# A relational graph network on one core: tail groups of 4 and 7 tiles, shared gather buffers, and accumulators that begin with the bias

## The chip, the cores and the metric

The kernel runs on one core of a Trainium2 chip. A core has five engines with their own instruction queues: TensorE (PE, matrix multiplications, with the loading of its stationary operand shown as PEld), VectorE (DVE), ScalarE (ACT), GpSimd (POOL) and SyncE (SP, which only issues transfers here). They work on SBUF, an on-chip memory of 128 partitions, and on PSUM, where TensorE writes its results, and wait for each other by semaphores. The metric is the time of one execution in microseconds. The kernel before takes 4633.61 us, the median of 10 runs (4629.92 to 4639.09).

## The reference

Two layers of a relational graph convolution over 12,500 nodes of 128 features and 200,000 edges of 10 relations, then a residual and a layer normalisation. The edges are sorted by destination. An edge's relation is the greatest of 10 of its 42 attributes.

```python
def _rgcn_layer(x, src, dst, edge_type, w_rel, root, bias):
    N = x.shape[0]
    seg = dst * NUM_REL + edge_type
    xs = x[src]
    sums = jax.ops.segment_sum(xs, seg, num_segments=N * NUM_REL)
    cnt = jax.ops.segment_sum(jnp.ones(seg.shape, x.dtype), seg, num_segments=N * NUM_REL)
    mean = (sums / jnp.maximum(cnt, 1.0)[:, None]).reshape(N, NUM_REL, -1)
    return jnp.einsum('nrd,rdo->no', mean, w_rel) + x @ root + bias

h = jax.nn.relu(_rgcn_layer(x, src, dst, edge_type, w_rel1, root1, b1))
x = _layernorm(x + _rgcn_layer(h, src, dst, edge_type, w_rel2, root2, b2))
```

So a layer gathers 200,000 rows of 512 bytes, averages them per node and relation, multiplies each average by its relation's 128x128 matrix, and adds the node's own row times `root` and a bias.

## The kernel before

**Tiles and groups.** A tile is 128 edges in order of destination; there are 1,563 tiles. Groups of 16 tiles (`G`) are the unit of work: 95 of them (`NS`), indices 0 to 94, and then a tail of 43 tiles in smaller groups. `groups` (L68 to L72) cuts it into 8, 8, 8, 8, 4, 4 and 3 tiles, indices 95 to 101.

**What a group does**, for each layer:
- `gather` (L464): one indirect transfer per tile, issued by POOL (L466), fetches the 128 source rows into a buffer `g` of 16 tiles. `gpool` has three such buffers, handed out in turn to the groups; a group of 8, 4 or 3 tiles takes a whole one too. The first gather of a group waits until PE is done with the group that had the buffer before, three groups back.
- `ones` (L475): per tile DVE builds a matrix `oh` (L481), with a column for each pair of relation and destination in the tile's window of 12 nodes, holding the edge's weight, and for the group `at` (L485), which places windows among 160 nodes. `dpool` has two buffers for `oh`.
- `sums` (L488): PE multiplies the gathered rows by `oh`, two instructions per tile (L495), into `zp`; ACT copies `zp` to `zs` (L509), one copy per four tiles. There is one `zp`.
- `project` (L514): for each half group of up to 8 tiles 10 relations are summed in `pp` (L521), two instructions each: 40 instructions for a group of 16, 20 for a smaller one. ACT copies the result to `ms` (L527, or L525 when the group is not a whole number of halves).
- `add` (L532): PE places the result among 160 nodes (L537) and DVE adds it to `acc` (L543), the accumulator of all nodes, at an offset read from memory. `pp` is also the name of that PSUM tile, and it has one buffer.

**Blocks of nodes.** When enough groups have been added that a block of nodes is complete (`done_after`, L79), it is finished: 23 blocks of 512 nodes, five of 128 and one of 84. `block_in` (L394) loads the block's rows and transposes them on PE (L407) and copies them on ACT (L409). `block_rows` (L412) adds the bias to the block's part of `acc` on DVE, giving `a` (L416), zeroes that part of `acc` in layer 0 (L418) so that layer 1 can use it, and lets PE add the rows times `root` (L421) and `a`, transposed by the identity (L422). In layer 0 (`hidden`) ACT applies the relu (L435) and SP stores the block to DRAM as `hD`; layer 1 gathers from there. In layer 1 (`final`) DVE and ACT do the residual and the layer normalisation (L447 to L457) and SP stores the output.

**The order** is that of the program as `layer` (L545) writes it out. In the groups of 16 the stages of several groups overlap: a group's gathers run while its predecessors are multiplied and projected. In the tail (`end`) each group is multiplied, projected and added before the next is begun, except that the one-hots of the next group come ahead. The large blocks end with the first groups of the tail; the six small ones are finished after indices 93, 94, 95, 97, 99 and the last. The last block's inputs are loaded early (`ready`). Layer 1's first gather needs the whole of `hD`.

**The beginning.** The edges' data are brought to one column per tile (`sources`, `places`, `types`, `count`), in chunks of 128 tiles, the first ahead of the loop and the others between groups. Ahead of the loop the accumulator is zeroed by 25 copies on ACT (L615), and `weights_in` loads the matrices and biases.

A second, general way through the problem follows behind a flag (from L647), for edges that don't fit the windows. It isn't taken with these inputs.

Of the kernel before, what the change touches and what calls it, by code (L numbers as in the profile page):

```python
# [9 lines left out]
F32 = mybir.dt.float32  # L10
BF16 = mybir.dt.bfloat16
I32 = mybir.dt.int32
AF = mybir.ActivationFunctionType
ALU = mybir.AluOpType
# [6 lines left out]
P = 128  # L21
# [5 lines left out]
G = 16  # L27
QB = 4
HT = 8
# [5 lines left out]
CT = 128  # L35
YB = 512
W = 128
GT = 125
# [5 lines left out]
def rgcn_resnorm_kernel(ctx: ExitStack, tc: tile.TileContext, x, src, dst, attr, w_rel1, root1, b1,  # L44
# [14 lines left out]
    nc = tc.nc  # L59
    N, C = x.shape  # L60
    E = src.shape[0]
    D = attr.shape[1]
    CE = CT * P
    NT = -(-E // P)
# [3 lines left out]
    groups = [(t, G) for t in range(0, NS * G, G)]  # L68
    t = NS * G
    while t < NT:  # L70
        groups.append((t, min(HT if NT - t > 3 * QB else QB, NT - t)))
        t += groups[-1][1]  # L72
    NG = len(groups)
    NPAD = N + SW
# [12 lines left out]
        return min(a + n for a, n in groups if a + n >= t)  # L87

    HALF = NT * P - E
    assert C == P and E % GT == 0 and 0 < HALF < P and NT % CT and 1 < groups[-1][1] < groups[-2][1]  # L90

    const = ctx.enter_context(tc.tile_pool(name="const", bufs=1))
    dram = ctx.enter_context(tc.tile_pool(name="dram", bufs=1, space=DRAM))
    fin = ctx.enter_context(tc.tile_pool(name="fin", bufs=1))
# [12 lines left out]
    gpool = fast.enter_context(tc.tile_pool(name="gpool", bufs=RING))  # L107
# [6 lines left out]
    ident = const.tile([P, P], F32, name="ident")  # L114
# [29 lines left out]
    def later(ins):  # L144

        for f in ahead:
            tc.add_manual_dep(ins.ins, f.ins.name, behind, reason="the first counts wait for it")
# [3 lines left out]
    def then(engine, ins):  # L151

        if engine in loaded:
            loaded.remove(engine)
            tc.keep_in_program_order(ins)
        return ins
# [10 lines left out]
    def sources(c):  # L167
        p = chunk_rows(c)
        s_i = prep.tile([P, P], I32, name="s_i")
        rows_from(s_i, src, c, 0, P)  # L170
        s_f = prep.tile([P, P], F32, name="s_f")
        early(c, nc.vector.tensor_copy(s_f[:p], s_i[:p]))
        return to_edges(idxE, s_f, c)
# [54 lines left out]
    acc = const.tile([P, NPAD], F32, name="acc")  # L228
# [10 lines left out]
    while k < NG:  # L239
        t, n = groups[k]  # L240
# [4 lines left out]
        m = n if q < NG else n - 1  # L245
# [8 lines left out]
    def places():  # L254
        early(0, nc.vector.tensor_scalar(bt, bt, 0, N - 1, op0=ALU.max, op1=ALU.min))
        early(0, nc.vector.tensor_copy(b8, b8_i))
        pw = ps_f.tile([P, YB], F32, name="pf")
        for h in range(2):
            nc.tensor.matmul(pw[:HR, h * NG:(h + 1) * NG], rank[:, h * HR:(h + 1) * HR], b8, start=True, stop=True)
        nc.vector.tensor_scalar(place, pw[:HR, :2 * NG].rearrange("p (h g) -> p h g", h=2), within, None, op0=ALU.add)  # L260
        nc.vector.tensor_reduce(wide[:HR], place, axis=AX.XY, op=ALU.max)

    wsb, rsb, bsb = [], [], []

    def weights_in():
        for l, (wr, ro, bi) in enumerate(((w_rel1, root1, b1), (w_rel2, root2, b2))):
            t = const.tile([P, NREL, C], F32, name=f"w{l}")
            later(nc.sync.dma_start(t, wr.rearrange("r d o -> d r o")))
            wsb.append(t)
            t = const.tile([P, C], F32, name=f"root{l}")  # L270
            later(nc.sync.dma_start(t, ro))
            rsb.append(t)
            t = const.tile([P, 1], F32, name=f"b{l}")
            later(nc.sync.dma_start(t, bi.rearrange("(c o) -> c o", o=1)))
            bsb.append(t)
# [102 lines left out]
    def block(k):  # L378
        n0 = starts[k]
        n = (starts + [N])[k + 1] - n0  # L380
        return n0, n, [(t, min(P, n - t * P)) for t in range(-(-n // P))]
# [12 lines left out]
    def block_in(k, l):  # L394
# [14 lines left out]
        nc.scalar.activation(fT[:, :n], pt[:, :n], AF.Copy)  # L409
        return xb, fT  # L410

    def block_rows(fT, k, l):  # L412

        n0, n, subs = block(k)
        a = fin.tile([P, YB], F32, name="a")
        nc.vector.tensor_scalar(a[:, :n], acc[:, n0:n0 + n], bsb[l], None, op0=ALU.add)  # L416
        if l == 0:
            nc.vector.memset(acc[:, n0:n0 + n], 0.0)  # L418
        pr = ps_f.tile([P, 4, C], F32, name="pf")
        for t, h in subs:  # L420
            nc.tensor.matmul(pr[:h, t, :], fT[:, t * P:t * P + h], rsb[l], start=True, stop=False)  # L421
            nc.tensor.matmul(pr[:h, t, :], a[:, t * P:t * P + h], ident, start=False, stop=True)  # L422
        return pr

    def spans(k):
# [3 lines left out]
    def hidden(k, ready):  # L429

        xb, fT = ready
        pr = block_rows(fT, k, 0)
        hb = fin.tile([P, 4, C], F32, name="hb")
        for p, s in spans(k):
            nc.scalar.activation(hb[:p, s], pr[:p, s], AF.Relu)  # L435
        rows_dma(hb, hD, k, True)
# [24 lines left out]

    HELD = "clamped to a node on the chip"

    def gather(table, t0, n):  # L464
        g = gpool.tile([P, G, C], F32, name="g")
        return g, [then("POOL", nc.gpsimd.indirect_dma_start(  # L466
            out=g[:, j, :], out_offset=None, in_=table, in_offset=bass.IndirectOffsetOnAxis(
                ap=idxE[:, t0 + j:t0 + j + 1], axis=0))) for j in range(n)]
# [139 lines left out]
        yield  # L608

    sources(1)  # L610
    zero = fin.tile([P, YB], F32, name="a")
    nc.vector.memset(zero, 0.0)
    for a in range(0, NPAD, YB):
        m = min(NPAD - a, YB)
        nc.scalar.activation(acc[:, a:a + m], zero[:, :m], AF.Copy)  # L615
    places()
    for _ in chain(types(0), count(0)):
        pass
    weights_in()
    todo = []  # L620
    for c in range(1, NCH):
        s = [as_steps(sources, c + 1)] if c + 1 < NCH else []
# [31 lines left out]
    def relations(ty, dt):  # L654
        o = gp.tile([P, RS], dt, name="rel" + ("b" if dt == BF16 else "f"))
        nc.vector.tensor_scalar(o, iota[:, :RS], ty, None, op0=ALU.is_equal)
        return o
# [53 lines left out]
    def g_before(table):  # L711
        def before(e, ty):
            rel = relations(ty, F32)
            pt = gps.tile([P, P], F32, name="gpt")
            nc.tensor.transpose(pt[:RS], rel, ident)
            relT = gp.tile([RS, P], F32, name="grelT")
            nc.scalar.activation(relT, pt[:RS], AF.Copy)
            v = gp.tile([P, 1], F32, name="gv")
            nc.vector.memset(v, 0.0)
            s_i = gp.tile([P, 1], I32, name="gs_i")  # L720
            nc.sync.dma_start(s_i[:GT], src[ds(e, GT)].rearrange("(e o) -> e o", o=1))
            g = gp.tile([P, C], F32, name="gg")
            nc.vector.memset(g, 0.0)
            nc.gpsimd.indirect_dma_start(out=g[:GT], out_offset=None, in_=table,
                                         in_offset=bass.IndirectOffsetOnAxis(ap=s_i[:GT], axis=0))
            return relT, v, g, ty
        return before
# [12 lines left out]
    def g_messages(l):  # L740
        def messages(st):
            _, v, g, ty = st
            nc.vector.tensor_scalar(v, v, 1.0, None, op0=ALU.max)
            nc.vector.reciprocal(v, v)
            pm = gps.tile([P, C], F32, name="gpm")
            for r in range(NREL):
                vr = gp.tile([P, 1], F32, name="gvr")
                nc.vector.tensor_scalar(vr, ty, float(r), v, op0=ALU.is_equal, op1=ALU.mult)
                gr = gp.tile([P, C], F32, name="ggr")
                nc.vector.tensor_scalar(gr, g, vr, None, op0=ALU.mult)  # L750
                pt = gps.tile([P, P], F32, name="gpt")
                nc.tensor.transpose(pt, gr, ident)
                gT = gp.tile([P, P], F32, name="ggT")
                nc.scalar.activation(gT, pt, AF.Copy)
                nc.tensor.matmul(pm, gT, wsb[l][:, r, :], start=(r == 0), stop=(r == NREL - 1))
            ms = gp.tile([P, C], F32, name="gms")
            nc.scalar.activation(ms, pm, AF.Copy)
            return ms
        return messages
# [8 lines left out]
    with tc.If(flag > 0):  # L768
        nc.vector.memset(acc, 0.0)
        each_tile(lambda e, ty: relations(ty, BF16), [(g_count, None)])  # L770
        nc.sync.dma_start(counts, acc[:RS])
        for l, (table, finish) in enumerate(((x, hidden), (hD, final))):
            nc.vector.memset(acc, 0.0)
            each_tile(g_before(table), [(g_look, g_messages(l)), (g_add, None)])
            for k in range(NBLK):
                finish(k, block_in(k, l))
# [26 lines left out]
```

## Time and profile before

| What | Value |
|---|---|
| median of 10 runs | 4633.61 us (4629.92 to 4639.09) |
| profiled execution | 4627.56 us, of which 4625.8 us span |
| mean granted TensorE clock | 0.753 |
| layer 0's tail, from the first gather of index 95 to the first gather of layer 1 | 2229.01 to 2323.13, 94.1 us |
| layer 1's tail, from the first gather of index 95 to the end | 4519.94 to 4625.8, 105.9 us |
| gathers per layer | 1563, one per 1.25 us within a burst |

Times in the profile are microseconds from the span's start. A burst is a run of gathers on POOL with no wait in it. In the page, an engine's line gives busy time, share of the span and instructions, and the chain of work that ended last is given as shares by engine and by line. An answer by windows has one line per stretch of time: its ends, its length, the busy time of the engine with the number of instructions begun in it, the clock that was granted to TensorE as a share of the full one, the mean busy share of the core's transfer engines, and GB/s. A line of the waits has the engine and line that waited, what it waited for, the time in all, how many times, and the longest.

### The profile page before, as it was taken

How to read it: one execution, taken by the hardware profiler on the slowest of the kernel's cores; microseconds unless marked ns; L12 is line 12 of the kernel's file. 1: busy time of each engine (PE TensorE's matmuls, PEld its weight loads, DVE VectorE, ACT ScalarE, POOL GpSimd, SP SyncE). 2: the span in 40 equal slices, each digit the busy share in tenths (PEclk: the TensorE clock that was granted, in tenths of full speed). 3: DMA queues.
4: the chain of work that ended last, by engine and by line, in shares of the span. 5: the costliest groups of instructions: out<-in, count | busy, mean ns of one | idle time of the engine just before them, and what ended most of it. 6: DMA issues, size and time to landing. Idle time of an engine off the chain costs nothing.

```text
span 4625.8 us, 43799 instructions
## 1 busy us (share of the span) xinstructions
PE 2748.8 (59%) x16206; PEld 2451.9 (53%) x16206; DVE 1513.8 (33%) x4660; ACT 530.0 (11%) x1142; POOL 2965.7 (64%) x3142
## 2 busy tenths in 40 slices
PE   3655655655656566566736556666565565656666
PEld 2445555555555555555625555555555555555556
DVE  4243333333333333333322222222222223222233
ACT  1111111111111111111101111111111111111111
POOL 6666666666666666666566666666666666666663
PEclk7677777777777777777867777777777777777778
DMA  4122222222122121111111111211121112111111
GB/s 138 52 71 78 63 66 80 63 64 76 55 78 75 52 80 51 57 50 52 48 51 51 53 53 52 60 53 53 53 60 53 53 53 60 53 49 53 57 54 40
DMA packets 180538, 278.99 MB, mean 60 GB/s; under 512 B 55608, under 2 KB 127175, under 8 KB 177191
## 3 DMA queue, kind: packets, MB, share of 16 engines
q0 software_dynamic: 100032, 205.07, 15.4%
q1 hardware_dynamic: 78577, 71.03, 4.8%
q8 instruction: 132, 2.16, 0.2%
q14 instruction: 89, 0.73, 0.0%
q10 hardware_dynamic: 1708, 0.01, 0.0%
HBM read 262.28 MB, written 13.60 MB: 60 GB/s over the span
## 4 chain that ended last, share of the span: by engine, by line
issue 26%; PE 26%; POOL 25%; another core or an unknown queue 18%; DVE 5%; ACT 1%; DMA 0%; DVEq 0%; ACTq 0%; POOLq 0%
POOL g L466 25%; PE pp L521 14%; PE zp L495 8%; DVE oh L481 3%; PE pp L537 2%; PE pf L422 1%; PE pf L421 1%; ACT zs L509 1%; PE pf L366 0%; PE pf L364 0%; DVE acc L543 0%; DVE at L485 0%; DVE eqb L362 0%; PE pf L407 0%
## 5 line engine op out<-in xcount | busy, mean ns | idle before, releaser
L521 PE MATMUL pp<-w,zs 128*96 128x128 f32 x7880 | 1507.7, 349 | 1068.3 <-issue 970.7
L466 POOL DMA_INDIRECT g<-in_x_dram,idxE x1563 | 1479.9, 947 | 821.2 <-issue 428.0
L466 POOL DMA_INDIRECT g<-hD,idxE x1563 | 1482.9, 949 | 814.5 <-issue 455.9
L521 PEld LDWEIGHTS pp<-w,zs 128*96 128x96 f32 x7880 | 1324.3, 221 | 1262.1 <-issue 1155.4
L481 DVE TENSOR_SCALAR oh<-bank,keyE,wE 128x120 f32<-128x120 f32 x3126 | 1003.1, 391 | 1104.1 <-remote 966.4
L495 PE MATMUL zp<-oh,g 128*128 128x120 f32 x6252 | 924.4, 299 | 311.9 <-issue 288.7
L495 PEld LDWEIGHTS zp<-oh,g 128*128 128x128 f32 x6252 | 866.1, 215 | 326.7 <-issue 317.7
L509 ACT ACTIVATE zs<-zp 128x480 f32<-128x480 f32 (+1 forms) x782 | 385.5, 574 | 2525.8 <-remote 2356.2
L543 DVE TENSOR_TENSOR acc<-acc,pp 128x160 f32 x204 | 65.6, 322 | 1231.4 <-remote 743.7
L537 PE MATMUL pp<-at,ms 96*128 96x160 f32 (+1 forms) x788 | 172.0, 343 | 276.5 <-issue 232.6
L537 PEld LDWEIGHTS pp<-at,ms 96*128 96x128 f32 (+1 forms) x788 | 122.9, 202 | 316.2 <-issue 261.9
L527 ACT ACTIVATE ms<-pp 96x256 f32<-96x256 f32 (+1 forms) x198 | 74.5, 376 | 921.5 <-remote 544.0
L422 PE MATMUL pf<-ident,a 128*128 128x128 f32 x392 | 95.3, 323 | 97.8 <-issue 64.8
L362 DVE TENSOR_TENSOR eqb<-pf,kh 128x1344 bf16<-128x1344 f32 (+2 forms) x65 | 100.3, 1550 | 114.0 <-PE pf L366 65.9
L485 DVE TENSOR_SCALAR at<-bank,place 96x160 f32<-96x160 f32 x394 | 133.0, 371 | 0.0
L422 PEld LDWEIGHTS pf<-ident,a 128*128 128x128 f32 x392 | 70.7, 222 | 105.0 <-issue 66.0
L421 PE MATMUL pf<-root,fT 128*128 128x128 f32 x388 | 90.5, 315 | 36.3 <-issue 29.1
L447 DVE TENSOR_TENSOR v<-pf,xb 128x512 f32<-128x512 f32 (+1 forms) x28 | 17.4, 620 | 252.0 <-remote 246.1
L421 PEld LDWEIGHTS pf<-root,fT 128*128 128x128 f32 x388 | 70.7, 224 | 42.3 <-issue 33.5
L364 PE MATMUL pf<-eqb,identb 128*128 128x512 bf16 (+2 forms) x130 | 53.2, 409 | 15.8 <-DVE eqb L362 10.0
L435 ACT ACTIVATE hb<-pf 128x512 f32<-128x512 f32 (+2 forms) x29 | 15.4, 532 | 371.3 <-remote 266.1
L366 PE MATMUL pf<-eqb,identb 128*128 128x512 bf16 (+2 forms) x130 | 53.2, 409 | 3.6 <-issue 3.3
(107 smaller groups left out, 454.9 us busy)
## 6 DMA issues: line engine op xcount, KB each, us to landing
m<-in_edge_attr_dram SPq DMA_DIRECT2D x24, 1344.0 KB
g<-in_x_dram,idxE POOLq DMA_INDIRECT x1563
g<-hD,idxE POOLq DMA_INDIRECT x1563
xb<-in_x_dram SPq DMA_DIRECT2D x46, 256.0 KB
hD<-hb SPq DMA_DIRECT2D x23, 256.0 KB
hb<-hD SPq DMA_DIRECT2D x23, 256.0 KB
out_dram<-o SPq DMA_DIRECT2D x23, 256.0 KB
w<-in_L_gnn_w_rel_dram SPq DMA_DIRECT2D x2, 640.0 KB
```

Of the source, the lines that this page charges most:

```text
L362: nc.vector.tensor_tensor(eq[:p], kp[:p, None, :R].to_broadcast([p, DB, R]), fore, op=ALU.is_equal)
L421: nc.tensor.matmul(pr[:h, t, :], fT[:, t * P:t * P + h], rsb[l], start=True, stop=False)
L422: nc.tensor.matmul(pr[:h, t, :], a[:, t * P:t * P + h], ident, start=False, stop=True)
L466: return g, [then("POOL", nc.gpsimd.indirect_dma_start(out=g[:, j, :], out_offset=None, in_=table, in_offset=bass.IndirectOffsetOnAxis(ap= ...
L481: then("DVE", nc.vector.tensor_scalar(oh[:, j, :], iotaP[:, :KW], keyE[:, t:t + 1], wE[:, t:t + 1], op0=ALU.is_equal, op1=ALU.mult))
L485: nc.vector.tensor_scalar(at[:, h, :], iotaP[:HR], place[:, h, k:k + 1], None, op0=ALU.is_equal)
L495: m = nc.tensor.matmul(zp[:, j // QB, j % QB * KW:(j % QB + 1) * KW], g[:, j, :], oh[:, j, :], start=True, stop=True)
L509: then("ACT", nc.scalar.activation(zs[:, :, b * QB:b * QB + m, :], zp[:, b, :m * KW].rearrange("c (j r n) -> c r j n", r=NREL, n=WN), AF.C ...
L521: nc.tensor.matmul(po[:m * WN, h], zs[:, r, h * HT:h * HT + m].rearrange("c j n -> c (j n)"), wsb[l][:, r, :], start=(r == 0), stop=(r == ...
L527: nc.scalar.activation(ms[:, :n // HT], po[:HR, :n // HT], AF.Copy)
L537: nc.tensor.matmul(pa, ms[:m * WN, h], at[:m * WN, h], start=(h == 0), stop=(h == len(parts) - 1))
L543: nc.vector.tensor_tensor(acc[:, s], acc[:, s], pa, op=ALU.add)
```

## The change

Three things are changed.

- The tail's groups: a group of 8 while more than 12 tiles are left, one of 4 while more than 8 are left, then the rest. That makes 8, 8, 8, 8, 4, 7 (indices 95 to 100), 101 groups in place of 102.
- `gather`: a buffer `g` of 16 tiles is taken only when the group begins at a multiple of 16 tiles; other groups write to the rest of the last one. So indices 95 and 96, 97 and 98, and 99 and 100 share a buffer, and only the first of each pair waits for a buffer, that of group 92, 93 and 94.
- The bias: the accumulator is filled with the first layer's bias (25 activations on ACT with the bias as operand, behind `weights_in` now), `block_rows` gives the accumulator itself to PE, and in layer 0 ACT refills the block's part with the second layer's bias behind PE's reading it, ahead of the relu. The addition L416 and the memset L418 go. `zero` becomes a constant tile. The general way's memset becomes a copy of the bias.

```diff
     while t < NT:
-        groups.append((t, min(HT if NT - t > 3 * QB else QB, NT - t)))
+        n = NT - t
+        groups.append((t, HT if n > HT + QB else QB if n > HT else n))
         t += groups[-1][1]
...
+    zero = const.tile([P, YB], F32, name="zero")
+
     def block_rows(fT, k, l):
 
         n0, n, subs = block(k)
-        a = fin.tile([P, YB], F32, name="a")
-        nc.vector.tensor_scalar(a[:, :n], acc[:, n0:n0 + n], bsb[l], None, op0=ALU.add)
-        if l == 0:
-            nc.vector.memset(acc[:, n0:n0 + n], 0.0)
         pr = ps_f.tile([P, 4, C], F32, name="pf")
         for t, h in subs:
             nc.tensor.matmul(pr[:h, t, :], fT[:, t * P:t * P + h], rsb[l], start=True, stop=False)
-            nc.tensor.matmul(pr[:h, t, :], a[:, t * P:t * P + h], ident, start=False, stop=True)
+            nc.tensor.matmul(pr[:h, t, :], acc[:, n0 + t * P:n0 + t * P + h], ident, start=False, stop=True)
+        if l == 0:
+            nc.scalar.activation(acc[:, n0:n0 + n], zero[:, :n], AF.Identity, bias=bsb[1])
         return pr
...
+    shared = {}
+
     def gather(table, t0, n):
-        g = gpool.tile([P, G, C], F32, name="g")
+
+        o = t0 % G
+        if not o:
+            shared["g"] = gpool.tile([P, G, C], F32, name="g")
+        g = shared["g"][:, o:o + n]
         return g, [then("POOL", nc.gpsimd.indirect_dma_start(
             out=g[:, j, :], out_offset=None, in_=table, in_offset=bass.IndirectOffsetOnAxis(
                 ap=idxE[:, t0 + j:t0 + j + 1], axis=0))) for j in range(n)]
...
     sources(1)
-    zero = fin.tile([P, YB], F32, name="a")
     nc.vector.memset(zero, 0.0)
-    for a in range(0, NPAD, YB):
-        m = min(NPAD - a, YB)
-        nc.scalar.activation(acc[:, a:a + m], zero[:, :m], AF.Copy)
     places()
     for _ in chain(types(0), count(0)):
         pass
     weights_in()
+    for a in range(0, NPAD, YB):
+        m = min(NPAD - a, YB)
+        nc.scalar.activation(acc[:, a:a + m], zero[:, :m], AF.Identity, bias=bsb[0])
```

## The prediction

> **What bounds the kernel now.** I read the page's busy times and its chain first, then TensorE's (PE's) instruction counts window by window, then the waits and the chain at the ends of the layers. In the page, no engine is busy more than two thirds of the span, and the chain names PE, the gathers and time without a cause in equal parts.
>
> ```profile
> PE 2748.8 (59%) x16206; PEld 2451.9 (53%) x16206; DVE 1513.8 (33%) x4660; ACT 530.0 (11%) x1142; POOL 2965.7 (64%) x3142
> issue 26%; PE 26%; POOL 25%; another core or an unknown queue 18%; DVE 5%; ACT 1%; DMA 0%; DVEq 0%; ACTq 0%; POOLq 0%
> ```
>
> A steady group takes about 23.05 us: 16 gathers, one per 1.25 us (19.7 us), and some 3.3 us in which GpSimd (POOL) waits until PE frees a gather buffer. The next view is PE alone in one such period, cut at 6.5 us, 13 us and at the end of the gathers; its columns are length, PE busy (instructions), granted clock, DMA share, GB/s.
>
> ```profile
> 1017.60:1024.10 6.50, 6.50 (x37) 0.66 0.14 40
> 1024.10:1030.60 6.50, 4.54 (x38) 1.00 0.21 58
> 1030.60:1037.30 6.70, 1.66 (x5) 0.63 0.19 54
> 1037.30:1040.64 3.34, 1.67 (x6) 0.50 0.06 20
> ```
>
> What to see: 75 matmuls start in the first 13 us of the burst of gathers, then 5 in 6.7 us. A burst twice as long, at 4052.40, shows the same as one step: 79 in 13 us, then 16 in 26.77.
>
> ```profile
> 4052.40:4065.40 13.00, 11.09 (x79) 0.84 0.17 48
> 4065.40:4092.17 26.77, 5.60 (x16) 0.53 0.19 53
> ```
>
> So the number of matmuls that PE gets through depends on how long the gathers run without a break. The end of a layer has bursts of 8, 8, 8, 8, 4, 4, 3 gathers (in layer 1 the fourth and fifth join to 12). The same view there, first the last steady period, then two stretches of 23.05 us and one of 13.75 us from the start of the first short burst, for layer 0 and layer 1, and one step of 8 tiles late in the tail:
>
> ```profile
> 2205.96:2229.01 23.05, 14.74 (x88) 0.80 0.17 49
> 2229.01:2252.06 23.05, 17.23 (x128) 0.90 0.16 46
> 2252.06:2275.11 23.05, 18.93 (x141) 0.85 0.15 43
> 2275.11:2288.86 13.75, 7.53 (x55) 0.86 0.24 69
> 4496.89:4519.94 23.05, 14.86 (x88) 0.80 0.16 46
> 4519.94:4542.99 23.05, 20.03 (x152) 0.91 0.16 47
> 4542.99:4566.04 23.05, 16.50 (x106) 0.78 0.18 49
> 4566.04:4579.79 13.75, 9.61 (x62) 0.88 0.15 44
> 2295.81:2301.98 6.17, 5.44 (x42) 1.00 0.17 49
> ```
>
> With short bursts PE starts 106 to 152 matmuls in the time in which it starts 88 with a burst of 16; late in the tail it does 42 in 6.17 us, 6.8 per us. Who waits in layer 0's tail (2225 to 2326):
>
> ```profile
> POOL g L466 <- PE zp L495: 21.8, 5, 10.3
> PE pp L521 <- ACT zs L509: 4.4, 5, 1.8
> PE pf L422 <- DVE a L416: 1.9, 2, 1.1
> ```
>
> POOL waits for PE; no row of PE in that tail names a gather. The last gather there ends at 2304.51, the last accumulator add starts at 2319.25. Thus PE's own work, at the pace that the gathers leave it, sets the end of each layer. The steady stage has nothing in it that the change touches on its chain.
>
> **The change, part by part.** All sums are against the profiled execution, 4627.56 us (span 4625.8 and 1.8 around it); it lies 6.05 us below the median 4633.61, which is added at the end.
>
> *Buffers.* Groups 95+96, 97+98 and 99+100 share a buffer, so the bursts at the end of a layer become 16, 16 and 11. POOL's queue keeps three waits, for the matmuls L495 of groups 92, 93 and 94, and loses four. In layer 0 the waits were 2.14, 5.22, 10.32, 2.05, 2.75 and 1.41 us, but as nothing on PE waits for gathers, taking them away ends nothing sooner. The price is PE's pace. The first burst still starts at 2229.01 and runs 19.7 us; the second starts when group 93's matmuls are done. Those were done at about 2240.6; by the steady pattern (3.3 us behind a burst) I expect 2252. Group 94 then frees its buffer at 2275 instead of 2255.5, and the third burst lasts 13.75 us. So I give the first two stretches the 88 matmuls of the steady period ahead of each tail, the nearest row, instead of the 128 and 141 (152 and 106) found, and the third the 71 that is the mean of four long bursts' first 13.75 us (61 to 79). Layer 0 then is behind by 40 + 53 - 16 = 77 matmuls, layer 1 by 64 + 18 - 9 = 73. At 6.8 per us that is 11.3 and 10.7 us: +22.0. Bounds of this term inside the theory: six steady periods had 77 to 88, the third stretch 61 to 79, which gives 134 to 214 matmuls in all, 19.7 to 31.5 us. Outside it the bound is nothing lost. What is queued behind is everything: VectorE's (DVE's) one-hots of group 95 wait for the same matmuls of 93, ScalarE's (ACT's) copies for PE.
>
> By the Trainium skill, "SBUF — State Buffer", section "SBUF: two separate sides", a DMA can't be slowed by a compute operation nor the other way round, and PE never waits on another's port. By that rule longer bursts would cost PE nothing, this term would be 0 and the whole sum -6.7. The row of 5 matmuls in 6.7 us shows PE and the gathers bound together in some way, port or not, and I go by the row.
>
> Part of the slow pace is the clock (1.00 falling to 0.50). The skill's "TensorE: Matmul & The Clock Gate", Part 1, has the clock halve after an idle window of about 3.4 us; if only the granted clock differed (0.90, 0.85, 0.91, 0.78 against 0.80), the term would be about 2.6 + 1.4 + 2.8 + 0 = 6.7 us and the sum about nought. But half a clock makes a pace of half, not a tenth.
>
> *Groups.* Adds of successive 4-tile groups are 4.65 and 4.84 us apart, so one group fewer takes 4.75 us off. The last has 7 tiles instead of 3: the 3-tile step took 4.30, the 8-tile step 6.28 (add at 2299.18 to 2305.46), so a tile adds (6.28 - 4.75) / 4 = 0.4 and the 7-tile step takes 5.9: +1.6. Together -3.15 per layer, -6.3. PE sets both; 1 us either way.
>
> *Bias.* The 29 additions L416 per layer (0.48 us for a block of 512, 0.28 for 128) and 29 memsets L418 (0.48, 0.17) leave DVE. Beside the steady stage they were hidden: the wait of POOL that ends each period is PE's. At the ends they lie on the path: layer 0's last add 2319.25, a 2319.70, matmul 2320.00, and layer 1's 4617.46, 4617.81, 4618.13; without a, about 0.33 us less each. Elsewhere PE waited 1.9 us for a in layer 0's tail. In exchange, layer 0's refill of acc on ACT comes ahead of hb; by ACT's other rows it costs 0.52 us for 512 and 0.27 for 128, the last one on the path. Per layer between 0.1 and 1.9 gained; I take 0.5, near the rows of the last block: -1.0. The queued store of hb and the copies of zs behind the refill wait 0.27 us, once per small block; included.
>
> At the start 25 fills of 0.52 us (11.83 to 24.82) move behind the weights' loads and the copy L356 (33.19). They then end at about 47 us; ACT's next instruction is the first copy L509 at 78.4, before which it waited 44.8 us for PE, so that wait hides them (without it they would cost their 13 us). ACT's table load (1.28 us, 10.54) may fall in front of the copy: 0 to 1.3, I take +0.6. No DMA of SP's queue moves past another one that PE waits for.
>
> Sum: 22.0 - 6.3 - 1.0 + 0.6 = +15.3, so 4642.9 profiled and **4649 us** as a median. The likeliest case's own range: 19.7 - 6.3 - 3.8 + 0 = +9.6 to 31.5 - 6.3 - 0.2 + 1.3 = +26.3, 4643 to 4660.
>
> **Rivals.**
> 1. *No loss of pace* (the other side). PE's slow pace at the end of a burst may only show that it has no more work. Then the term of 22 goes and the groups and the bias leave -6.3 - 1.0 + 0.6 = -6.7: 4627. For it: in tail bursts of 8 PE went 18 matmuls in the last 3.19 us. Against it: in the 32-gather burst PE had a group waiting and started 16 in 26.77 us. It decides as soon as PE keeps above 120 matmuls in the first shared burst's 23 us.
> 2. *POOL sets the tail after all.* The removed waits sum to 23.9 us in layer 0 and 30.1 in layer 1; if half came back, -27 and 4607. Against it: no row of PE waits for a gather, and the gathers ended 14.7 us before the last add.
> 3. *Half of it.* Only the first shared burst loses: 40 and 64 matmuls, 5.9 + 9.4 = 15.3, so +8.6 and 4642, because PE is slow in the later stretches already (106 in layer 1).
>
> **How the numbers follow.** About 0.2% (9 us) is what a measurement of this kernel can tell from no change. The likeliest case gets 0.58 (slower 0.54, same 0.04), the first rival 0.15 (4620 to 4632: same 0.10, faster 0.05), the second 0.14 (faster), the third 0.13 (same 0.07, slower 0.06). That makes faster 0.19, same 0.21, slower 0.60. The range runs from 4624, in the middle of the first rival, to 4663, a little above the likeliest case's end; outside it are the second rival and a few hundredths at either end.
>
> **What would show it.** In the changed profile: bursts of 16, 16 and 11 gathers with waits of about 3 us between them; PE at 80 to 95 matmuls in each of the two stretches of 23 us; 25 us more from 2229 to group 94's matmuls, of which the rest of the tail wins back some; the step before last one group shorter; L416 and L418 gone, L422 directly behind the add. I am wrong if POOL's wait behind a shared burst is near nothing, if PE's count there stays above 120, or if the steady period moves from 23.05 us, where 0.1 us per period would be 19 us over both layers.

## The result and the profile after

The changed kernel takes 4660.3 us (median of 8, 4657.94 to 4668.14), the kernel before 4633.45 (28 runs by then). The ratio is 1.006, with a 95% interval of 1.0052 to 1.0069: 26.85 us slower. The profiled execution of the changed kernel took 4656.66 us with a span of 4654.9, 29.1 more than before. In the changed file the lines have moved by a few: the gathers are L473, the one-hot products L502, the projection L528, the placing L544, the add L550, the accumulator's product L421 and ACT's refill L423.

Where the 29.1 us lie is read off the starts of gathers that have the same place in both programs:

| Stretch | before | after | difference |
|---|---|---|---|
| start to the first gather of the tail of layer 0 | 2229.01 | 2238.35 | +9.3 |
| tail of layer 0, to layer 1's first gather | 94.12 | 102.25 | +8.1 |
| layer 1 up to its tail | 2196.81 | 2198.54 | +1.7 |
| tail of layer 1, to the end | 105.9 | 115.8 | +9.9 |

The first view of the changed kernel is PE by windows: the last steady period, the two shared bursts with the waits behind them, and 13.75 us from the start of the third burst, for each layer (length, PE busy and instructions, granted clock, DMA share, GB/s).

```profile
2215.36:2238.35 22.99, 15.07 (x88) 0.72 0.18 49
2238.35:2261.32 22.97, 13.61 (x86) 0.80 0.16 46
2261.32:2284.42 23.10, 13.65 (x81) 0.80 0.16 46
2284.42:2298.17 13.75, 11.60 (x72) 0.75 0.27 73
4516.18:4539.14 22.96, 14.64 (x87) 0.72 0.17 46
4539.14:4562.09 22.95, 14.74 (x83) 0.72 0.16 46
4562.09:4585.18 23.09, 13.23 (x88) 0.80 0.20 57
4585.18:4598.93 13.75, 10.34 (x70) 0.87 0.26 70
```

Where the kernel before started 128, 141, 152 and 106 matmuls, this one starts 86, 81, 83 and 88. Those are steady periods in number and in length: POOL waits 3.27 and 3.40 us behind the two shared bursts of layer 0, 3.24 and 3.39 in layer 1, as it does behind nearly every burst of 16. The third burst has 72 and 70.

The end of layer 0 in the changed kernel's timeline (start, length, engine, line, operation):

```profile
2336.90 0.32 DVE L550 TENSOR_TENSOR acc<-acc,pp 128x160 f32 x1 [1.45 <-PE pp L544]
2337.28 0.45 PE L421 MATMUL pf<-ident,acc 128*84 128x128 f32 x2 [0.41 <-DVE acc L550]
2337.76 0.36 ACT L423 ACTIVATE acc<-zero,b 128x84 f32<-128x84 f32 x1 [1.49 <-PE pf L421]
2338.03 0.25 ACT L436 ACTIVATE hb<-pf 84x128 f32<-84x128 f32 x1
2340.60 0.95 POOL L473 DMA_INDIRECT g<-hD,idxE  x1 [42.74 <-DMA hD<-hb]
```

PE follows the last add after 0.38 us in place of 0.75, and the refill takes 0.27 of that back ahead of the relu. From the last add to layer 1's first gather it is 3.70 us, before 3.88.

The one place outside the tails where the two kernels part for good is around 365 us. The burst before begins 3.1 us later in the changed kernel (344.94 and 341.85), this one 9.6 us later (374.61 and 365.02). The waits of the changed kernel's PE from 340 to 376, and of its POOL from 323 to 378:

```profile
PE pp L544 <- ACT ms L534: 12.1, 1, 12.1
PE pf L408 <- ACT hb L436: 4.0, 1, 4.0
...
POOL g L473 <- PE zp L502: 10.0, 1, 10.0
```

The kernel before has no wait of PE for ACT there, and POOL's wait at the same place is 3.45 us. The changed kernel's ACT and PE in that window:

```profile
346.58 0.74 ACT L423 ACTIVATE acc<-zero,b 128x512 f32<-128x512 f32 x1
347.19 0.62 ACT L436 ACTIVATE hb<-pf 128x512 f32<-128x512 f32 x1
...
367.66 0.38 ACT L534 ACTIVATE ms<-pp 96x256 f32<-96x256 f32 x1 [18.06 <-remote]
```

```profile
347.86 1.11 PE L408 MATMUL pf<-ident,xb 128*128 128x128 f32 x4 [4.05 <-ACT hb L436]
348.77 6.56 PE L528 MATMUL pp<-w,zs 128*96 128x128 f32 x40
...
368.10 1.44 PE L544 MATMUL pp<-at,ms 96*128 96x160 f32 x4 [12.10 <-ACT ms L534]
```

PE's transposes of the next block wait for the relu, which now stands behind the refill, and all 40 projections of the group stand behind the transposes. In the kernel before, 18 of the 40 went ahead of the transposes (L407 there):

```profile
324.42 1.11 PE L521 MATMUL pp<-w,zs 128*96 128x128 f32 x8 [0.41 <-issue]
...
328.93 0.38 PE L521 MATMUL pp<-w,zs 128*96 128x128 f32 x2
...
342.46 1.91 PE L521 MATMUL pp<-w,zs 128*96 128x128 f32 x8
344.17 1.11 PE L407 MATMUL pf<-ident,xb 128*128 128x128 f32 x4
345.08 3.13 PE L521 MATMUL pp<-w,zs 128*96 128x128 f32 x22
```

There the copy to `ms` came at 350.40, 8.5 us after the burst's start. Here it comes 22.7 us after it, 3.0 us behind the burst's last gather. The records show the projections at 355.3 at the latest, but ACT, idle since 349.61, begins its copy of them only at 367.66. By the program the copy reads nothing else; the profile names what released it only as "remote", another core or a queue that it does not know. So PE's records within this burst seem to run some 12 us ahead of what has been finished.

### The profile page after: what moved, and what is told of

Its sections match the earlier page's. It is cut to its first block, busy times and chain, and to the rows that moved or that the text cites. A ratio compares the mean times of both kernels' runs of the same rounds, so it can differ in the third digit from the quotient of the medians.

```text
span 4654.9 us, 43649 instructions
## 1 busy us (share of the span) xinstructions
PE 2782.9 (60%) x16162; PEld 2483.1 (53%) x16162; DVE 1493.5 (32%) x4569; ACT 544.5 (12%) x1169; POOL 2962.2 (64%) x3142
## 3 DMA queue, kind: packets, MB, share of 16 engines
q0 software_dynamic: 100032, 205.07, 15.4%
## 4 chain that ended last, share of the span: by engine, by line
PE 44%; issue 27%; another core or an unknown queue 22%; DVE 7%; ACT 1%; DMA 0%; DVEq 0%; ACTq 0%
PE pp L528 23%; PE zp L502 13%; DVE oh L488 5%; PE pp L544 3%; PE pf L421 1%; PE pf L420 1%; ACT zs L516 1%; PE pf L367 1%; PE pf L365 1%; DVE at L492 0%; DVE acc L550 0%; PE pf L408 0%; DVE st L451 0%; DVE o L458 0%
## 5 line engine op out<-in xcount | busy, mean ns | idle before, releaser
L528 PE MATMUL pp<-w,zs 128*96 128x128 f32 x7840 | 1522.1, 352 | 1072.4 <-issue 946.1
L528 PEld LDWEIGHTS pp<-w,zs 128*96 128x96 f32 x7840 | 1333.1, 224 | 1271.7 <-issue 1141.0
L473 POOL DMA_INDIRECT g<-hD,idxE x1563 | 1479.4, 947 | 821.3 <-issue 436.9
L473 POOL DMA_INDIRECT g<-in_x_dram,idxE x1563 | 1479.9, 947 | 814.4 <-issue 431.0
L502 PE MATMUL zp<-oh,g 128*128 128x120 f32 x6252 | 925.2, 301 | 291.1 <-issue 257.2
L502 PEld LDWEIGHTS zp<-oh,g 128*128 128x128 f32 x6252 | 872.0, 217 | 301.1 <-issue 280.3
L550 DVE TENSOR_TENSOR acc<-acc,pp 128x160 f32 x202 | 64.9, 321 | 1237.6 <-remote 762.0
L544 PE MATMUL pp<-at,ms 96*128 96x160 f32 (+2 forms) x784 | 175.9, 350 | 294.1 <-issue 240.4
L544 PEld LDWEIGHTS pp<-at,ms 96*128 96x128 f32 (+2 forms) x784 | 126.1, 208 | 335.2 <-issue 269.6
L421 PE MATMUL pf<-ident,acc 128*128 128x128 f32 x392 | 106.4, 357 | 89.8 <-issue 66.6
L421 PEld LDWEIGHTS pf<-ident,acc 128*128 128x128 f32 x392 | 80.4, 252 | 99.5 <-issue 73.3
L423 ACT ACTIVATE acc<-zero,b 128x512 f32<-128x512 f32 (+2 forms) x29 | 19.0, 655 | 400.6 <-remote 289.0
```

What stands on the lines that cost most here:

```text
L421: nc.tensor.matmul(pr[:h, t, :], acc[:, n0 + t * P:n0 + t * P + h], ident, start=False, stop=True)
L473: return g, [then("POOL", nc.gpsimd.indirect_dma_start(out=g[:, j, :], out_offset=None, in_=table, in_offset=bass.IndirectOffsetOnAxis(ap= ...
L502: m = nc.tensor.matmul(zp[:, j // QB, j % QB * KW:(j % QB + 1) * KW], g[:, j, :], oh[:, j, :], start=True, stop=True)
L528: nc.tensor.matmul(po[:m * WN, h], zs[:, r, h * HT:h * HT + m].rearrange("c j n -> c (j n)"), wsb[l][:, r, :], start=(r == 0), stop=(r == ...
L544: nc.tensor.matmul(pa, ms[:m * WN, h], at[:m * WN, h], start=(h == 0), stop=(h == len(parts) - 1))
```

## The experiments

The runs fell on several chips, each with its own runs of the kernel before beside them, so the ratios are the measure. The chips differ more than the kernels do, as will be seen. The first four runs fell together on one chip, the "second chip" below; the changed kernel was not run there.

### Each part alone, and the parts without long bursts

**The groups alone.** The kernel before with only

```diff
-        groups.append((t, min(HT if NT - t > 3 * QB else QB, NT - t)))
+        n = NT - t
+        groups.append((t, HT if n > HT + QB else QB if n > HT else n))
```

> Only the tail's groups, 4 and 7 instead of 4, 4, 3; buffers and bias as before. Theory (PE's pace under long bursts of gathers costs the time; a group fewer saves): bursts of gathers stay short, so 3.15 us less per layer, 6.3 in all, ratio 0.9986. Rival (a tail with 7 tiles last costs, because everything of the last group lies on the chain): 1.000 to 1.002.

Measured: 1.0004 (0.9989 to 1.0020), on a chip on which the kernel before takes 4731.55 us. The gain that was expected, 0.9986, is a little outside the interval.

**The buffers alone.** The kernel before with only

```diff
     def gather(table, t0, n):
-        g = gpool.tile([P, G, C], F32, name="g")
+        o = t0 % G
+        if not o:
+            shared["g"] = gpool.tile([P, G, C], F32, name="g")
+        g = shared["g"][:, o:o + n]
```

> Only the shared buffers, groups and bias as before; bursts become 16, 16 and 11. Theory: PE starts about 88 matmuls in the 23 us of each of the first two bursts, and the time is 22 us longer (19 to 27), ratio 1.0047. Rival (the bias part makes the loss, the changed tails only look longer because of it): within 5 us of before, ratio 0.999 to 1.001.

Measured: 1.0048 (1.0032 to 1.0065), 22.7 us more (15 to 31).

**The bias alone.** The changed kernel with the old groups and the old `gather`.

> Only the accumulators that begin with the bias. In the changed profile the stretch ahead of layer 0's tail is 9.3 us longer and the steady stretch of layer 1 1.7 us. Theory (the bias part reorders PE's queue ahead of the tails): +8 to +12 us, ratio 1.002. Rival (those 11 us come from the other two parts by way of the order that the scheduler gives the whole program, or differ from run to run): within 3 us of before.

Measured: 1.0012 (0.9999 to 1.0026), 5.7 us more, with an interval that begins at nothing. In its profile POOL waits 10.33 us before the burst that begins at 381.00, the same burst as the one at 365; on the same chip the groups alone wait 4.48 us there.

**The whole change with the waits back.** The changed kernel, buffers shared, gathers of the tails held in the order written, and

```diff
+        if k > NS:
+            tc.add_manual_dep(gathers[0].ins, last_zp[k - 3], whole, reason="as if it had a buffer of its own")
```

> The changed kernel with its shared buffers, but each tail group's first gather waits for the matmuls of the group three before, as if it had a buffer of its own; bursts are 8, 8, 8, 8, 4, 7 again. Theory (length of the bursts): the 22 us come back and the time is 3 to 7 us above before, ratio 1.001. Rival (sharing itself, two groups' tiles in one buffer, holds PE): the time stays at that of the changed kernel, ratio 1.006.

Measured: 1.0005 (0.9990 to 1.0020).

The views that carry these verdicts are PE by windows again, the first two stretches of 23.05 us of each tail: first the groups alone, then the buffers alone, then the whole change with its waits.

```profile
2274.64:2297.69 23.05, 16.84 (x122) 0.87 0.15 41
2297.69:2320.74 23.05, 16.53 (x107) 0.73 0.16 43
4592.37:4615.42 23.05, 17.65 (x126) 0.87 0.18 46
4615.42:4638.47 23.05, 17.09 (x122) 0.85 0.17 47
```

```profile
2283.84:2306.89 23.05, 14.70 (x82) 0.72 0.18 46
2306.89:2329.94 23.05, 14.87 (x83) 0.80 0.17 46
4624.08:4647.13 23.05, 11.90 (x83) 0.82 0.18 46
4647.13:4670.18 23.05, 15.47 (x86) 0.72 0.18 46
```

```profile
2287.87:2310.92 23.05, 15.77 (x118) 0.87 0.18 47
2310.92:2333.97 23.05, 18.50 (x119) 0.72 0.14 41
4623.69:4646.74 23.05, 16.59 (x122) 0.87 0.16 43
4646.74:4669.79 23.05, 18.03 (x112) 0.73 0.18 49
```

With bursts of 8 PE starts 107 to 126 matmuls, with bursts of 16 it starts 82 to 86, and putting the waits back into the shared buffers brings 112 to 119 again and the time with them. So it is not the sharing of a buffer that holds PE, it is that POOL is no longer stopped. (Putting the waits back shortens the bursts at the same time, so the two are not told apart by this run.) The three parts alone add to 1.9 + 22.7 + 5.7 = 30.3 us on this chip, beside 26.85 for the whole on the first.

The groups alone seem to miss their gain for a like reason. The step of the last group of 8, from add to add, took 6.28 us in layer 0 of the kernel before; here it is 12.17 (2351.85 to 2364.02). A burst of 7 gathers ran beside it, 2347.57 to 2356.01. PE's products for that step are recorded until 2353.5, and ACT's copy of them starts only here, 1.6 us behind the burst's last gather:

```profile
2357.65 1.03 ACT L510 ACTIVATE zs<-zp 128x480 f32<-128x480 f32 x2 [2.55 <-remote]
```

In the changed kernel the gathers are over by then and that step takes 6.07. The other two kernels on this chip fit: with the waits back a burst of 7 runs beside the step too (2358.79 to 2367.2), and it takes 12.89; with the bias alone, which has the old groups of 4, 4 and 3, it takes 7.01.

### A pause in place of a wait, the refill, and what the gathers are

**Pauses.** The changed kernel with fills of a scratch tile by POOL ahead of each tail group's gathers, and the order held as above:

```diff
+        if end and k > NS:
+            for _ in range(3):
+                d = nc.gpsimd.memset(idle, 0.0)
+                tc.add_manual_dep(d.ins, in_order[-1].ins.name, behind, reason="in the order written")
+                in_order.append(d)
```

> The changed kernel, buffers shared and no wait for PE added; before the gathers of each tail group but the first, POOL fills a scratch tile three times, about 3.3 us in which no gather is issued. Theory (an unbroken burst is what slows PE, and a pause is enough to let it recover): the ratio falls from 1.006 to 1.001 to 1.003, although POOL has more to do. Rival (PE needs the wait itself, for the earlier waits kept POOL from getting ahead and so bunching its gathers): no better than the changed kernel, 1.005 to 1.008.

**The refill on DVE.** The bias alone with

```diff
-            nc.scalar.activation(acc[:, n0:n0 + n], zero[:, :n], AF.Identity, bias=bsb[1])
+            nc.vector.tensor_scalar(acc[:, n0:n0 + n], zero[:, :n], bsb[1], None, op0=ALU.add)
```

> The bias part alone, but DVE refills the accumulator with the second bias instead of ACT. Theory (ACT's refill ahead of the relu holds the relu's PSUM buffer, and PE's next transposes and the projection behind them slip into the slow part of a burst): the stall at 365 us in layer 0 is gone and the time is 3 to 7 us below the bias part alone, ratio 0.9995 to 1.0005. Rival (the order of DVE's and PE's queues without the addition makes it): as with the bias part alone, 1.0010 to 1.0015.

**Plain transfers in the tails.** The changed kernel with

```diff
+        if t0 >= NS * G:
+            return g, [nc.gpsimd.dma_start(g, table[0:n * P].rearrange("(j p) c -> p j c", p=P))]
```

> The changed kernel, but in the tails each group's gathers are one plain transfer of as many rows in order of node, issued by POOL, with the same buffers and waits; the gather by source is left out for the tail's edges. Theory (the gathers slow PE): PE goes at 6 to 7 matmuls per us all through the tails, the first 23 us see 120 to 155 instead of about 88, and each tail is 15 to 25 us shorter, ratio 0.993 to 0.998. Rival (PE's slow stretches come from its own order and waits): the tails keep their length within 5 us, ratio 1.004 to 1.008.

**A pause in every burst.** The kernel before with one fill between the eighth and the ninth gather of each group of 16:

```diff
+        if not end and k > 2:
+            d = nc.gpsimd.memset(idle, 0.0)
+            tc.add_manual_dep(d.ins, gathers[HT - 1].ins.name, behind, reason="after half a group")
+            for x in gathers[HT:]:
+                tc.add_manual_dep(x.ins, d.ins.name, behind, reason="after the pause")
```

> The kernel before with one fill of a scratch tile by POOL, about 1.1 us without a gather, in the middle of each burst of 16. Theory, its strong form (any pause brings PE back to pace): the wait of 3.3 us behind each burst shrinks by more than the pause, the period falls from 23.05 to 21.5 to 22.5 us, ratio 0.94 to 0.98. Its weak form (PE recovers only when a pause is longer than about 1.5 us): the period grows by the pause, to 23.8 to 24.2 us, ratio 1.03 to 1.05.

These four ran together on another chip, and there the kernel before takes 3948.25 us in place of 4633. Measured: pauses in the tails 1.0056 (1.0042 to 1.0070); the refill on DVE 0.9991 (0.9982 to 1.0000); plain transfers 0.9973 (0.9963 to 0.9983); a pause in every burst 1.0384 (1.0368 to 1.0400), with a period of 20.83 us, 20.0 and the 0.83 by which the gap with the fill (1.13) is longer than a usual one (0.30). On this chip the rows in which POOL waits for PE come to 1.2 us in all with the refill on DVE (four of the usual gaps of 0.3) and to 1.5 us with a pause in every burst: the period without pauses is 20.0 us, sixteen gathers with next to nothing between them. So none of these could test what a pause does for a PE that is slow, or whether the refill on DVE takes away the stall at 365 us; no stall is there to be taken away. Where a ratio lies in a range given ahead (the pauses in the rival's, the plain transfers in the theory's), it does not speak for it. They show what a pause costs where POOL is the bound: about all of it.

Two things can be read from them even so. First, the order in PE's queue. The changed kernel has the same order at the block of the stall on the first chip and on one with periods of 20 us (four transposes, 40 projections, six one-hot products, from 347.86 and from 255.54), so orders can be compared across chips. With the refill on DVE all 40 projections stand behind the transposes there too:

```profile
256.24 0.64 PE L407 MATMUL pf<-ident,xb 128*128 128x128 f32 x4
256.72 0.38 PE L364 MATMUL pf<-eqb,identb 128*128 128x512 bf16 x1
256.94 4.53 PE L521 MATMUL pp<-w,zs 128*96 128x128 f32 x40
```

So it is not the place of the refill that moved them there. Second, the plain transfers: PE by windows from the start of layer 0's tail, where no gather runs.

```profile
1905.91:1928.96 23.05, 21.12 (x166) 0.89 0.47 147
1928.96:1952.01 23.05, 19.44 (x158) 1.00 0.10 27
```

These counts are to be set beside those of the changed kernel with its gathers on such a chip, which come next.

### The changed kernel on such a chip

**The changed kernel itself**, to see what it does there.

> The changed kernel itself, to set beside the kernel before on one more chip; on one chip POOL went through a whole layer without waiting for PE, and the period was 20.0 us instead of 23.05. Theory: where the periods are 23 us, PE is slowed by the bursts and the ratio is 1.005 to 1.007; where they are 20 us, POOL has no wait to lose, shared buffers do nothing, and the ratio is 0.998 to 1.001. Rival (the loss has nothing to do with PE's pace under the bursts): 1.006 on either.

**The pauses once more**, the same kernel.

> The same kernel as the one with POOL's pauses of 3.3 us between the tail groups. Theory: where the periods are 23 us, pauses bring PE back to pace and the ratio is 1.001 to 1.003; where they are 20 us, the pauses lie on the chain, five of 3.15 us per layer, and it is 1.005 as seen. Rival: as the changed kernel or above where the periods are 23 us, 1.006 to 1.009.

**What costs nothing, together**: the groups of 4 and 7 and the bias with DVE's refill, no shared buffers.

> The parts that cost nothing, together: the tail groups 4 and 7, the accumulators that begin with the bias, refilled by DVE; no shared buffers. Theory: where the periods are 23 us, 3 to 6 us less than before from the group that is missing and up to 3 either way from the bias, ratio 0.998 to 1.000; where they are 20 us, the last group's 7 tiles lie behind the last gather, 0.999 to 1.000. Rival (the bias part costs 5 to 9 us wherever the refill lies): 1.000 to 1.002.

**Two fills in every burst**, the kernel with the pause in each burst and a second fill behind the first.

> The kernel before with two fills of a scratch tile by POOL, about 2.2 us without a gather, in the middle of each burst of 16. Where the periods of before are 23 us: if a pause alone brings PE back to pace, PE makes its 84 matmuls within the period, the wait behind the burst goes, and the period is 22.0 to 22.6 us, ratio 0.96 to 0.985; if PE comes back only by waiting for PE's own work, the pause is added and the period is 24.5 to 25.3, ratio 1.06 to 1.10. Where the periods are 20.0 us, the pause is added in full, 22.2 us, ratio about 1.08 to 1.10; the question stays open there.

All four fell on chips with periods of 20 us (before: 3947.7 and 3950.82). Measured: the changed kernel 0.9986 (0.9977 to 0.9995), so it is faster there; the pauses 1.0056 (1.0042 to 1.0070), as on the other such chip; the parts together 0.9986 (0.9977 to 0.9995), 3942.37 us beside 3942.11 for the changed kernel; two fills 1.0778 (1.0760 to 1.0796).

The changed kernel on this chip: the whole program's longest waits (engine and line, what it waited for, time in all, times, longest), and PE in the last 20 us ahead of layer 0's tail and in the two stretches of 23.05 us of the tail.

```profile
POOL g L473 <- issue: 930.3, 3012, 12.7
...
PE zp L502 <- DMA g<-hD,idxE: 786.5, 93, 13.8
PE zp L502 <- DMA g<-in_x_dram,idxE: 695.1, 92, 10.2
```

```profile
1885.00:1905.00 20.00, 11.59 (x78) 0.76 0.19 54
1905.08:1928.13 23.05, 21.72 (x162) 0.84 0.26 74
1928.13:1951.18 23.05, 19.38 (x159) 1.00 0.28 80
```

Here PE waits for gathers, 1,482 us in all, and POOL has only its own pauses of 0.3 us between gathers. In the tail POOL issues 43 gathers on end, in this kernel and in the one with a buffer per group, and beside them PE starts 162 and 159 matmuls in 23 us. Without gathers it was 166 and 158, so on this kind of chip the gathers take next to nothing from PE. The same instructions beside bursts of 16 gathers gave 86 and 81 on the first chip. On the first chip the waits of the kernel before read otherwise:

```profile
PEld pp L521 <- issue: 1155.4, 1040, 2.8
PE pp L521 <- issue: 970.7, 975, 2.6
...
POOL g L466 <- remote: 520.7, 159, 7.7
POOL g L466 <- PE zp L495: 169.5, 34, 19.2
```

There PE stands still over and over with no cause that the profile names ("issue"), and POOL waits: in 34 waits the row names PE, in 159 it names no engine, and by the program these are waits for PE's products of the group three before.

## Why the prediction was right, and where it was not

**Direction and range: right.** 4660.3 lies in 4624 to 4663, just above the top of the likeliest case's own 4643 to 4660. The point, 4649, was 11 us short. The two tails account for +18.0 us of the profiled difference, for which the sum had +14.8. The stretches ahead of them add +11.0, for which it had +0.6 and which it had no mechanism for. That the time stays within the range in spite of them is luck: the range was wide for other reasons.

**PE's pace under shared bursts: right in mechanism and size.** I gave each shared burst 88 matmuls and 22.0 us for both layers. The profile has 86, 81, 83 and 88 with 72 and 70 in the third, and the buffers alone cost 22.7 us (15 to 31). The waits put back into the shared buffers leave 1.0005 on the same chip. That shows that letting POOL run on without its waits is the cause on such a chip, and the counts show that PE gets less done meanwhile. It does not show by what means gathers slow PE.

**The rule that ports are separate** would have put this term at 0. By the Trainium skill, "SBUF — State Buffer", section "SBUF: two separate sides", DMA and compute can't slow each other. On chips with periods of 20 us the runs agree with it: 162 matmuls in 23 us beside an unbroken burst, 166 without gathers. On the two chips with periods of 23 us the measured 81 to 88 stand against it as a rule for the time. Whether anything is shared there, and what, no run shows. The granted clock, the other rule that I weighed, explains little: it is 0.80 in windows with 81 matmuls and 0.72 in one with 119.

**The groups: right in the changed kernel, wrong alone.** The step of 7 tiles takes 5.93 us in layer 0 (2330.97 to 2336.90), for which I had 5.9. The sum of a tail, 11.3 - 3.15 - 0.5 = +7.7 for layer 0 and 10.7 - 3.15 - 0.5 = +7.1 for layer 1, came out as +8.1 and +9.9. What I did not see is that the gain depends on the gathers being over: alone, with a burst of 7 beside the step of the last group of 8, it is given back.

**The bias at the ends of the layers: right.** PE follows the last add 0.37 us sooner in layer 0; in layer 1 it is 0.37 in place of 0.67 (the add at 4646.73, PE at 4647.10). The refill takes 0.27 back in layer 0.

**The bias elsewhere: the step that failed.** The sum had "Beside the steady stage they were hidden" and "+0.6" for the start; the runs show some 6 us that the bias part costs in layer 0's steady stage, and in the changed kernel 11 us outside the tails. The start itself is not to blame in the way I feared: the table load went to 31.50, the copy behind it came at 32.79 in place of 33.19, and the first burst after the waits begins 0.05 us later. The fills take 15.3 us, and ACT's wait for PE hides them. The loss comes at the second burst behind the start (+2.9) and at the burst at 365 us (+6.5); some goes and comes in small steps afterwards, and 9.3 are left at layer 0's tail. The second place is shown to belong to the bias part: the wait of 10 us stands there in the changed kernel (9.97), in the bias alone (10.33) and in the kernel with the waits back (10.16), and not before (3.45), with the groups alone (4.48) or with the buffers alone (4.32). I had counted the refill's 0.52 us, 0.74 as measured there, and had called what waits behind it included. I did not ask what becomes of the order in PE's queue. In the three kernels with the bias part on chips with periods of 23 us, all 40 projections of the group stand behind the four transposes that wait for the relu, and their copy comes only behind the burst, in which PE finishes little; in the kernel before 18 stood ahead. How long the relu holds PE up does not decide: PE waits 4.05 us for it in the changed kernel, 0.97 with the bias alone and 1.44 with the waits back, and POOL's wait is about 10 us in all three. Nor is it the refill that moved the projections, since they stand there with the refill on DVE too; so moving the refill need not take the stall away. That the order makes the stall is read from these windows and was not tested: no run had the bias part with the old order, and the run with DVE's refill fell on a chip without the stall. Nor was it found why the second burst comes 2.9 us later; the first add itself comes 2.3 us later there (92.91 and 90.63), in another place of DVE's queue. On the second chip this does not go with the bias: from the burst ahead of it to this one it is 30.3 us with the bias alone and 30.8 with the waits back, but 33.5 and 33.7 with the groups or the buffers alone. So these 2.9 us are not shown to be the bias part's.

**The rivals.** "No loss of pace" ends on the other side, and by the measure I gave (above 120 in the first shared burst) it falls on the first chip and holds on the chip with periods of 20 us on which the changed kernel ran: 162, ratio 0.9986. "POOL sets the tail after all" falls on the first chip, for taking away POOL's waits made the tails longer. "Half of it" falls with 86 and 81.

**What stays open.** What it is on a chip that makes PE slow under gathers, and whether it is the chip itself or something else that ran on it at the time, for no chip was seen in both ways; whether a pause without a wait for PE would bring it back, since the three kernels made to tell ran only where PE is not slow; whether the bias with DVE's refill, or the version of the parts together, is faster than before on a chip with periods of 23 us.

## What to carry to other kernels

A wait that looks like waste can be what holds two engines in step: before taking it away, count in the trace what the other engine gets done while it lasts and in the stretch after it. When instructions are added or taken away on one engine, compare the order of the other engines' instructions before and after too: here PE's projections and transposes changed places, which nobody had asked for. And a change that helps where one engine is the bound can hurt where another is: here the same change was 0.6% slower on one chip and 0.14% faster on another, so a ratio this small should be taken on more than one chip before it is trusted.

## What the runs showed of the hardware

- The same kernel takes 4633 us on one chip, 4731.55 on another and 3948 to 3951 on others. The granted clock of the kernel before is nearly the same, 0.753 on the first and 0.78 on the last, and a gather takes POOL 0.95 us on all. The transfers are no slower either: the gathers' packets took 15.4% of a span of 4625.8 us on the first (kernel before) and 18.2% of 3940.9 on one of the last (changed kernel), 712 and 717 us. What differs is PE beside the gathers, and with it the engine that sets the time: PE with POOL waiting in periods of 23 us, or POOL with PE waiting in periods of 20.
- The change is 0.6% slower on a chip of the first kind and 0.14% faster on one of the second; each is one chip.
- On the slow kind PE's records seem to run ahead of what is finished: projections recorded until 355.3 us were copied by an idle ACT only at 367.66, 3.0 us behind the last gather of the burst. A count of started matmuls is then a bound on what was done, and the waits of the engines behind PE are the surer reading.
